# Graph attention on one NeuronCore: when the weighted sums and the expert network of a tile are issued

## The chip, the cores and the metric

The kernel runs on one core of a Trainium2 chip. Time is device microseconds (us) of one execution. Each of the core's engines works through its own queue in order: PE (matrix products; PEld is its weight load), DVE (vector operations), ACT (activation functions and copies), POOL (here it issues the indexed loads, "gathers") and SP (here it issues the plain transfers). Semaphores order one engine's work after another's. [...]

## The reference

A graph has 3125 nodes with 256 features and 50000 edges sorted by destination. Two blocks follow one another, each with a residual sum: a relational graph convolution with a mixture of 16 experts, and then the block that this change touches:

```python
x = x + _L1_gnn_ref(_layernorm(x), ...)          # two graph attention layers, 8 heads of 32
x = x + _L1_ffn_ref(_layernorm(x)[None], ...)[0] # shared MLP + 2 of 4 experts, chosen by a softmax gate
```

One attention layer takes h = x W; for each edge a score e = leaky_relu(a_s[src] + a_d[dst], 0.2), less the largest score of the edges with the same destination; z = exp of that; and for each destination the sum of z h[src] over its edges, divided by the sum of z, plus a bias. Between the two layers stands an ELU. The last network is a shared MLP (256-256-128-256), four experts (256-128-64-256, two chosen per node) and the gate.

## The kernel before

The last part of the kernel holds 25 tiles of 125 destination nodes. A tile's edges fill 17 columns of 128 edges (CT = 17), in three parts of 6, 6 and 5 columns (PARTS). `layer` runs the 25 tiles as steps s, and in a step it works on several tiles at once: `new` is tile s+1, `now` is tile s, `old` is tile s-1 and `older` is tile s-2. It is called twice, for layer one and layer two of the attention; both calls stand in `tc.manual_schedule()`, in which each engine takes the instructions in the order in which the code emits them. Instructions that stand outside such a block are placed by the scheduler where it finds room. So the table `sel`, whose `iota` for POOL (L2052) and whose first vector operation (L2054) come after the first layer in the code, are executed inside the first layer.

What a step does, with the names used below:

- `fetch(new)`: POOL issues 17 gathers of 128 rows of h (line L113, a helper) into tiles g0, g1, g2, three buffers each. `fetch_rows`: SP loads index rows and carries for a tile further on.
- `scans(now)`: ACT copies the gathered scores (L1821), DVE runs two scans for the largest score (L1824, L1825), PE turns the ends (L1828, L1829). `hot_rows(new)`: two long ACT operations (L1873, L1874).
- `one_hot(now)` (DVE, L1837) builds the 0/1 matrix of edge to destination; `destinations(now)` (DVE, L1833) sums the looked-up a_d; `carried(now)` (DVE, L1842 to L1848, then PE L1851) passes the largest scores across lanes; `lookup(new)` (PE, L1880); `scores(now)` (eight DVE operations L1856 to L1864, then ACT Exp L1866 and three copies L1868).
- `weighted(w, k)` multiplies part k of the gathered rows by z on DVE (L1886, in place); `summed(w, k)` adds the rows up by destination with PE (L1894). The matrix products are in float32, and the profile counts two for each.
- `means(old)` (DVE, L1900 to L1906) divides and adds the bias; then four tails. In layer one: `elu_parts` (ACT, L1991 to L1993), `elu_sum` (DVE L1996, then PE transposes L1967), `next_hidden` (ACT L2001, PE L1776) and `keep_next` (ACT L1782, the transfer L1783 that writes the row table which layer two gathers from, five small DVE operations L927 to L931). In layer two only the first does anything: `residual` (DVE L2066 to L2071, ACT L2073 and L2074).

Layer two also runs the last network on pairs of tiles, hooked into the steps by a lag: `run(s, (lag, stage))` runs the stage on pair (s-2-lag)/2 where that is a whole number. `first_layers` (two layers of the shared MLP and four experts, PE L2099, and the gate's product L2104, L2106; each layer is followed by an ACT relu L2085), `second_layers` (PE L2122, L2127), `spread` (PE L2178, L2183), `third_layers` (PE L2196), `finish` (DVE L2200, output transfer L2201), `gates`, `choice` and `shares` (some twenty small DVE operations with two ACT Exp between, L2110 to L2172), `shared_out` (DVE L2187) and `normalize` (DVE L2078, ACT Sqrt L2079, DVE L2080, ACT L2082).

Before the change, odd steps run `first_layers`, `gates`, `choice` and `shares`, and even steps run `second_layers`, `spread`, `third_layers`, `finish`, `shared_out` and `normalize`. What is left after the last step is in `last`. Where no tile is left, a stage is skipped; at s = 25 only `old` and `older` remain.

Of the kernel before, what the change touches and what calls it, by code (L numbers as in the profile page):

```python
# [45 lines left out]
def gnn_kernel(ctx: ExitStack, tc: tile.TileContext, a: dict, out: bass.AP):  # L46
# [834 lines left out]
    def by_tiles(ctx, start_i, hard):  # L881
# [880 lines left out]
        with ExitStack() as st:  # L1762
# [4 lines left out]
            fx = fixed.tile([128, 128 + D], F32, name="fx")  # L1767
            iota_ps, bias_ps = fx[:, :R], fx[:R, 128:]
            nc.vector.tensor_copy(iota_ps, iota_r[:, :R])
# [3 lines left out]
            def hidden(wx, xT):  # L1773
                p = ps.tile([R, D + 2 * H], F32, name="p_x")
# [78 lines left out]
            def scores(w):  # L1853

                es, bw, ep, ad_e = w.es, w.bw, w.pe[:, :2], w.pe[:, 2]
                nc.vector.tensor_tensor(ep, ends[:, w.t, :, None, :].to_broadcast([128, 2, H, CT]),  # L1856
                                        w.pc[:, :, :, None].to_broadcast([128, 2, H, CT]), OP.add)
                nc.vector.tensor_max(bw, bw, ep[:, 0])
                nc.vector.tensor_max(bw, bw, ep[:, 1])
                nc.vector.tensor_add(ep, es, ad_e[:, None].to_broadcast([128, 2, H, CT]))  # L1860
                nc.vector.tensor_scalar(es, ep, 0.2, None, op0=OP.mult)
                nc.vector.tensor_max(es[:, 0], es[:, 0], ep[:, 0])
                nc.vector.tensor_max(ep[:, 1], es[:, 1], ep[:, 1])
                nc.vector.tensor_sub(es[:, 0], es[:, 0], ep[:, 1])  # L1864
                w.z = ad_e.rearrange("q h i -> q (h i)").rearrange("q (i h) -> q i h", h=H)
                nc.scalar.activation(heads(w.z), es[:, 0], AF.Exp)  # L1866
                for g, (i0, i1) in zip(w.g, PARTS):
                    nc.scalar.copy(g[:, :, D:], w.z[:, i0:i1])  # L1868
# [19 lines left out]
            def summed(w, k):  # L1888

                if k == 0:  # L1890
                    w.p = ps.tile([R, DX], F32, name="p_sum")
                i0, i1 = PARTS[k]
                for i in range(i0, i1):
                    m = nc.tensor.matmul(w.p, w.oh[:, i, :], w.g[k][:, i - i0, :], start=(i == 0), stop=(i == CT - 1))  # L1894
                added[k].append(m.ins)
# [12 lines left out]
            def layer(h_tab, ad, bias, tail1, tail2, tail3, tail4, slot=None, mid=None, end=None, last=None):  # L1908
# [7 lines left out]
                for s in range(-1, T + 1):  # L1916
# [47 lines left out]
            def transposed(x):  # L1964
                p = ps.tile([128, 2, R], F32, name="p_x")
# [120 lines left out]

            def first_layers(u):
                n = u.n * R
                xT = pool.tile([128, 2, 2 * R], F32, name="xT2", bufs=2)
                for i in range(u.n):  # L2090
                    nc.scalar.copy(xT[:, :, i * R:(i + 1) * R], transposed(u.xc[:, i, :]))
                u.h1 = pool.tile([128, 2, 2 * R], F32, name="sh1")
                u.g1 = pool.tile([128, n_e, 2 * R], F32, name="eh1")
                for w, dst, bias in ([(s1[:, :, m * 128:(m + 1) * 128], u.h1[:, m, :n], b1[:, m:m + 1])
                                      for m in range(2)] +
                                     [(e1[:, e], u.g1[:, e, :n], eb1[:, e:e + 1]) for e in range(n_e)]):
                    p = ps.tile([128, 2 * R], F32, name="p_x")
                    for k in range(2):
                        nc.tensor.matmul(p[:, :n], w[:, k, :], xT[:, k, :n], start=(k == 0), stop=(k == 1))  # L2099
                    relu(dst, p[:, :n], bias)  # L2100
                u.pg = ps.tile([R, 2, n_e], F32, name="p_x")
# [14 lines left out]
            def second_layers(u):  # L2116
# [3 lines left out]
                p = ps.tile([128, 2 * R], F32, name="p_x")  # L2120
                for k in range(2):
                    nc.tensor.matmul(p[:, :n], s2[:, k, :], u.h1[:, k, :n], start=(k == 0), stop=(k == 1))  # L2122
                relu(u.h2[:, :n], p[:, :n], b2)
                for half in range(2):
                    p = ps.tile([128, 2 * R], F32, name="p_x")
                    for k in range(2):
                        nc.tensor.matmul(p[:, :n], e2[:, 2 * half + k, :], u.g1[:, 2 * half + k, :n],  # L2127
                                         start=(k == 0), stop=(k == 1))
                    relu(u.g2[:, half, :n], p[:, :n], eb2[:, half:half + 1])
# [44 lines left out]
            def spread(u):  # L2174
                n = u.n * R
                p = ps.tile([n_e + 1, 2 * R], F32, name="p_x")
# [4 lines left out]
                u.pw = ps.tile([128, 2, 2 * R], F32, name="p_x")  # L2181
# [7 lines left out]
            def third_layers(u):  # L2189
                u.po = ps.tile([R, 2, D], F32, name="p_x")  # L2190
# [25 lines left out]
            def mid(s):  # L2216
                run(s, (4, finish), (1, gates))

            def end(s):
                run(s, (2, shared_out), (0, normalize), (1, choice), (1, shares))  # L2220

            def last():

                u, v, w = pairs[-3:]
                for step, p in ((third_layers, u), (finish, u), (first_layers, v), (normalize, w), (gates, v),
                                (second_layers, v), (choice, v), (shares, v), (first_layers, w), (gates, w),
# [5 lines left out]
            with tc.manual_schedule():  # L2232
                layer(tabs[1], ads[1], biases[1], residual, *[lambda w: None] * 3, slot, mid, end, last)
# [43 lines left out]
```

## Time and profile before

| what | value |
|---|---|
| median of 12 runs | 2643.36 us (2635.28 to 2649.27) |
| the profiled execution | 2629.63 us, of which the span is 2628.0 |
| granted PE clock, mean over the span | 0.867 |
| busy in the span: PE, DVE, ACT, POOL | 74%, 52%, 30%, 53% |
| gathers of attention layer one on POOL | from 1433.25 us of the span to 1968.4 |
| first gather of layer two | 2010.94 us |
| last gather of layer two | 2544.03 us |
| scans of the last tile of layer two | 2557.03 us |
| last operation of DVE | 2621.33 us |

The profile is one execution. Its times count from the first instruction. A line of a timeline gives the start, the duration (of the whole row where xN says several), engine, line of the code, operation, output and input names and, in brackets, how long the engine was idle before and what ended the wait. "issue" means that nothing that the profile shows was waited for.

### The profile page before, as it was taken

The numbers are of one execution on the slowest core, as the hardware profiler recorded it, in microseconds if no ns is written. First come the engines' busy times: TensorE is split into PE (matmuls) and PEld (weight loads), VectorE is DVE, ScalarE is ACT, GpSimd is POOL, SyncE is SP. The second block draws the span as 40 slices with busy tenths as digits, with TensorE's granted clock in tenths as the row PEclk, the third lists the DMA queues.
The fourth block names the chain that finished last, engine by engine and source line by source line (L and its number), as shares of the span: only waits on it lengthen the run. The fifth ranks groups of instructions, "written<-read, shape, count | busy, mean of one in ns | idle before, by whom it ended". The sixth has DMA issues, their size and how long they took to land.

```text
span 2628.0 us, 26960 instructions
## 1 busy us (share of the span) xinstructions
PE 1954.8 (74%) x8604; PEld 1426.9 (54%) x8604; DVE 1370.0 (52%) x2950; ACT 799.3 (30%) x1699; POOL 1396.6 (53%) x1445
## 2 busy tenths in 40 slices
PE   6667879999564999997985266666653578888887
PEld 2234545555443878886863144444442366666665
DVE  4068863332451441132114377777763677878783
ACT  2221122222021242242223233333331354445542
POOL 1106555775677704120015777777772777777750
PEclk9788999999776999998995588888886788989999
DMA  6524434554336737674634555555551554545430
GB/s 216 206 97 140 138 117 166 199 193 168 107 105 196 233 123 247 197 211 131 200 110 105 158 139 141 140 146 143 139 147 46 134 133 131 148 127 152 134 103 16
DMA packets 192309, 386.35 MB, mean 147 GB/s; under 512 B 39900, under 2 KB 112588, under 8 KB 186659
## 3 DMA queue, kind: packets, MB, share of 16 engines
q0 software_dynamic: 76464, 189.38, 27.6%
q1 hardware_dynamic: 104543, 184.41, 20.7%
q10 hardware_dynamic: 11152, 10.75, 1.2%
q8 instruction: 71, 1.16, 0.2%
q14 instruction: 79, 0.65, 0.1%
HBM read 294.45 MB, written 89.87 MB: 146 GB/s over the span
## 4 chain that ended last, share of the span: by engine, by line
PE 47%; DVE 17%; DMA 11%; POOL 11%; issue 9%; ACT 5%; SPq 0%; ACTq 0%; POOLq 0%; DVEq 0%
POOL g L113 10%; PE ph L1574 10%; PE p_tr L1266 10%; PE p_sum L1894 6%; PE sum L985 6%; PE py L1584 5%; DMA table_t<-tr 4%; DMA g<-h_tab_t,src_t 3%; PE p_x L2099 3%; DVE oh L1837 2%; DVE g L1886 2%; PE p_x L1776 1%; DMA g<-table_t,rg_t 1%; DVE to_lane L1165 1%; DMA xc<-xs_t 1%
## 5 line engine op out<-in xcount | busy, mean ns | idle before, releaser
L113 POOL DMA_INDIRECT g<-h_tab_t,src_t x850 | 808.6, 951 | 321.8 <-issue 265.6
L113 POOL DMA_INDIRECT g<-table_t,rg_t x450 | 447.7, 995 | 335.5 <-issue 114.8
L1894 PE MATMUL p_sum<-g,oh 128*125 128x264 f32 x1700 | 462.9, 432 | 14.4 <-DVE g L1886 11.7
L1894 PEld LDWEIGHTS p_sum<-g,oh 128*125 128x125 f32 x1700 | 356.3, 214 | 95.6 <-DVE g L1886 13.1
L1266 PE MATMUL p_tr<-w_rel_t,xT_t 128*125 128x512 f32 x800 | 370.8, 619 | 43.6 <-ACT tr L1269 43.6
L1574 PE MATMUL ph<-xcT,w 128*128 128x256 f32 x1312 | 310.6, 385 | 0.7 <-ACT xcT L1566 0.7
L985 PE MATMUL sum<-g,oh 128*125 128x256 f32 x900 | 240.5, 420 | 62.9 <-DMA g<-table_t,rg_t 29.4
L1266 PEld LDWEIGHTS p_tr<-w_rel_t,xT_t 128*125 128x125 f32 x800 | 155.3, 197 | 232.2 <-issue 176.2
L1886 DVE TENSOR_TENSOR g<-g,p_e 128x1536 f32<-128x1536 f32 x150 | 244.9, 1661 | 46.4 <-ACT g L1868 24.4
L1574 PEld LDWEIGHTS ph<-xcT,w 128*128 128x128 f32 x1312 | 249.3, 193 | 34.1 <-ACT xcT L1566 1.1
L1578 DVE TENSOR_TENSOR hT<-silu,ph 128x256 f32<-128x256 f32 x164 | 68.8, 420 | 378.4 <-ACT silu L1577 378.3
L1269 ACT COPY tr<-p_tr 125x512 f32<-125x512 f32 x200 | 115.0, 586 | 485.6 <-PE p_tr L1266 396.1
L985 PEld LDWEIGHTS sum<-g,oh 128*125 128x125 f32 x900 | 182.6, 208 | 110.7 <-issue 56.5
L113 POOL DMA_INDIRECT y<-ys,pos_i x50 | 61.2, 1224 | 330.3 <-DMA ys<-yc 218.7
L1584 PE MATMUL py<-w,hT 128*128 128x256 f32 x656 | 156.8, 382 | 0.2 <-DVE hT L1578 0.2
L1000 DVE TENSOR_TENSOR xr<-xr,sum 125x256 f32<-125x256 f32 x75 | 31.4, 418 | 240.5 <-PE sum L985 198.8
L1577 ACT ACTIVATE silu<-ph 128x256 f32<-128x256 f32 x164 | 62.7, 383 | 237.7 <-PE ph L1574 237.7
L1584 PEld LDWEIGHTS py<-w,hT 128*128 128x128 f32 x656 | 124.3, 191 | 17.2 <-DVE hT L1578 0.6
L1967 PE MATMUL p_x<-ident,en 125*128 125x125 f32 x50 | 16.7, 436 | 142.8 <-DVE en L1996 142.8
L1837 DVE TENSOR_TENSOR oh<-lo_t,fx 128x2125 f32<-128x2125 f32 x50 | 117.1, 2343 | 0.0
L1866 ACT ACTIVATE p_e<-es 128x136 f32<-128x136 f32 x50 | 14.4, 287 | 326.9 <-DVE es L1864 326.9
L1873 ACT ACTIVATE rows<-rows,minus_p 125x2176 bf16<-125x2176 bf16 x50 | 105.2, 2105 | 26.1 <-DMA g<-h_tab_t,src_t 17.5
(341 smaller groups left out, 2476.2 us busy)
## 6 DMA issues: line engine op xcount, KB each, us to landing
w<-in_L_ffn_w SPq DMA_DIRECT2D x123, 512.0 KB
table_t<-tr SPq DMA_DIRECT2D x44, 1000.0 KB
rows<-lo_rows_t SPq DMA_DIRECT2D x50, 531.2 KB
g<-h_tab_t,src_t POOLq DMA_INDIRECT x850, 2.9
xc<-xs_t SPq DMA_DIRECT2D x41, 256.0 KB
ys<-yc ACTq DMA_DIRECT2D x41, 256.0 KB
xs_t<-zero SPq DMA_DIRECT2D x9, 1024.0 KB
g<-table_t,rg_t POOLq DMA_INDIRECT x450, 5.3
```

Source lines behind the costliest of these rows:

```text
L113: return nc.gpsimd.indirect_dma_start(out=dst, out_offset=None, in_=table, in_offset=bass.IndirectOffsetOnAxis(ap=idx, axis=0))
L985: m = nc.tensor.matmul(r.p[:R, :D], r.oh[k][:, i - i0, :], r.g[k][:, i - i0, :], start=(i == r.parts[0][0]), stop=(i == r.parts[1][1] - 1))
L1266: m = nc.tensor.matmul(p, xT[:, k, t * R:(t + 1) * R], w_rel[:, k, r0:r0 + 2, :].rearrange("p r o -> p (r o)"), start=(k == 0), stop=(k == 1))
L1269: nc.scalar.copy(tr[:, 2 * q * D:(2 * q + 2) * D], p)
L1574: nc.tensor.matmul(p[:, which, :], u.w12[:, which, k, m * 128:(m + 1) * 128], u.xcT[:, k, :], start=(k == 0), stop=(k == 1))
L1578: nc.vector.tensor_mul(u.hT[:, m, :], s, p[:, 1, :])
L1584: nc.tensor.matmul(u.py[:, j, :], u.hT[:, m, j * 128:(j + 1) * 128], u.w3[:, m, :], start=(m == 0), stop=(m == nh - 1))
L1837: nc.vector.tensor_tensor(w.oh, lo[:, w.t, :, None].to_broadcast([128, CT, R]), iota_ps[:, None, :].to_broadcast([128, CT, R]), OP.is_equal)
L1873: nc.scalar.activation(w.rows, w.rows, AF.Abs, bias=minus_p[:R, :])
L1886: nc.vector.tensor_mul(g, g, w.z[:, i0:i1, :, None].to_broadcast([128, i1 - i0, H, HD]))
L1894: m = nc.tensor.matmul(w.p, w.oh[:, i, :], w.g[k][:, i - i0, :], start=(i == 0), stop=(i == CT - 1))
L2099: nc.tensor.matmul(p[:, :n], w[:, k, :], xT[:, k, :n], start=(k == 0), stop=(k == 1))
```

## The change

Attention: `weighted` and `summed` of a tile, which stood in the tile's own step (the last product one step later), all move into the next step. Part 0 stands between `one_hot` and `carried` there, parts 1 and 2 between `carried` and `destinations`. z no longer overwrites a part of the tile p_e; it gets its own place in the PSUM tile fx, in which the lane numbers (now in bf16) and the bias already lie. p_sum has one buffer instead of two, p_x three instead of two. The wait of the gathers on earlier sums names the tile three before.

Tails: `tail3` moves a step later, to just after `hot_rows`; `tail4` to after `tail1`, and `tail2` behind `tail4`.

Network: the transposes of `first_layers` become a stage of their own, `turned`. Odd steps now run `turned` (early), `shared_out` and `finish` (fill) and `first_layers` (slot). Even steps run `gates`, `choice` and `shares` (fill), `second_layers`, `spread` and `third_layers` (slot) and `normalize` (end). The output of two layers goes into one PSUM tile, all products of the two first, then the two relus.

```diff
-            iota_ps, bias_ps = fx[:, :R], fx[:R, 128:]
+            iota_ps, bias_ps = fx[:, :64].bitcast(BF16)[:, :R], fx[:R, 64:64 + D]
+            z_ps = fx[:, 64 + D:].rearrange("q (i h) -> q i h", h=H)
...
-                    if len(added[k]) >= 3:
-                        after_all(rows[0], [added[k][-3]])
+                    if w.t >= 3:
+                        after_all(rows[0], [added[k][w.t - 3]])
...
-                w.z = ad_e.rearrange("q h i -> q (h i)").rearrange("q (i h) -> q i h", h=H)
+                w.z = z_ps
...
-                    w.p = ps.tile([R, DX], F32, name="p_sum")
+                    w.p = ps.tile([R, DX], F32, name="p_sum", bufs=1)
...
+                    if older:
+                        tail3(older)
+                    if early and now:
+                        early(s)
                     if now:
                         one_hot(now)
-                        destinations(now)
-                    if older and s < T:
-                        tail4(older)
+                    if old:
+                        weighted(old, 0)
+                        summed(old, 0)
                     if now:
                         carried(now)
                     if old:
-                        summed(old, 2)
+                        for k in (1, 2):
+                            weighted(old, k)
+                            summed(old, k)
+                    if now:
+                        destinations(now)
+                    if fill:
+                        fill(s)
                     if new:
                         lookup(new)
                     if now:
                         scores(now)
                     if slot and now:
                         slot(s)
-                    if now:
-                        weighted(now, 0)
                     if old:
                         means(old)
                         tail1(old)
+                    if older:
+                        tail4(older)
+                    if old:
                         tail2(old)
+                    if s == T:
                         tail3(old)
-                    if now:
-                        summed(now, 0)
-                        weighted(now, 1)
-                        summed(now, 1)
-                        weighted(now, 2)
-                    if s == T:
-                        tail4(older)
                         tail4(old)
-                    if mid and now:
-                        mid(s)
                     if end and now:
                         end(s)
...
+            def turned(u):
+                n = u.n * R
+                p = ps.tile([128, 2, 2 * R], F32, name="p_x", bufs=3)
+                for i in range(u.n):
+                    for k in range(2):
+                        nc.tensor.transpose(p[:, k, i * R:(i + 1) * R], u.xc[:, i, k * 128:(k + 1) * 128], ident[:R, :R])
+                u.xT = pool.tile([128, 2, 2 * R], F32, name="xT2", bufs=2)
+                nc.scalar.copy(u.xT[:, :, :n], p[:, :, :n])
...
+                for c in range(0, len(made), 2):
+                    p = ps.tile([128, 2, 2 * R], F32, name="p_x", bufs=3)
+                    for j, (w, _, _) in enumerate(made[c:c + 2]):
+                        for k in range(2):
+                            nc.tensor.matmul(p[:, j, :n], w[:, k, :], xT[:, k, :n], start=(k == 0), stop=(k == 1))
+                    for j, (_, dst, bias) in enumerate(made[c:c + 2]):
+                        relu(dst, p[:, j, :n], bias)
...
-            def mid(s):
-                run(s, (4, finish), (1, gates))
+            def early(s):
+                run(s, (1, turned))
+
+            def fill(s):
+                run(s, (2, gates), (2, choice), (2, shares), (3, shared_out), (5, finish))
 
             def end(s):
-                run(s, (2, shared_out), (0, normalize), (1, choice), (1, shares))
+                run(s, (0, normalize))
```

In `last`, `turned` stands ahead of each `first_layers`; the order is otherwise the same, but for `normalize` of the last pair, which now stands ahead of the first layers of the pair before it.

More of the change, by code (lines that the diff above doesn't have):

```diff
@@ L1773, in hidden @@
             def hidden(wx, xT):
-                p = ps.tile([R, D + 2 * H], F32, name="p_x")
+                p = ps.tile([R, D + 2 * H], F32, name="p_x", bufs=3)
                 for k in range(2):
@@ L1906, in means, with layer @@
                 nc.vector.tensor_add(w.v, w.v, bias_ps)
-            def layer(h_tab, ad, bias, tail1, tail2, tail3, tail4, slot=None, mid=None, end=None, last=None):
+            def layer(h_tab, ad, bias, tail1, tail2, tail3, tail4, early=None, fill=None, slot=None, end=None,
+                      last=None):
                 nc.vector.tensor_copy(bias_ps, bias)
@@ L1964, in transposed @@
             def transposed(x):
-                p = ps.tile([128, 2, R], F32, name="p_x")
+                p = ps.tile([128, 2, R], F32, name="p_x", bufs=3)
                 for k in range(2):
@@ L2175, in spread @@
                 n = u.n * R
-                p = ps.tile([n_e + 1, 2 * R], F32, name="p_x")
+                p = ps.tile([n_e + 1, 2 * R], F32, name="p_x", bufs=3)
                 for i in range(u.n):
@@ L2189, in third_layers @@
             def third_layers(u):
-                u.po = ps.tile([R, 2, D], F32, name="p_x")
+                u.po = ps.tile([R, 2, D], F32, name="p_x", bufs=3)
                 for i in range(u.n):
@@ L2214, in slot @@
                 run(s, (1, first_layers), (2, second_layers), (2, spread), (4, third_layers))
-            def mid(s):
-                run(s, (4, finish), (1, gates))
+            def early(s):
+                run(s, (1, turned))
+            def fill(s):
+                run(s, (2, gates), (2, choice), (2, shares), (3, shared_out), (5, finish))
             def end(s):
-                run(s, (2, shared_out), (0, normalize), (1, choice), (1, shares))
+                run(s, (0, normalize))
             def last():
                 u, v, w = pairs[-3:]
-                for step, p in ((third_layers, u), (finish, u), (first_layers, v), (normalize, w), (gates, v),
-                                (second_layers, v), (choice, v), (shares, v), (first_layers, w), (gates, w),
+                for step, p in ((third_layers, u), (finish, u), (turned, v), (normalize, w), (first_layers, v), (gates, v),
+                                (second_layers, v), (choice, v), (shares, v), (turned, w), (first_layers, w), (gates, w),
                                 (spread, v), (shared_out, v), (choice, w), (shares, w), (second_layers, w),
@@ L2232, in by_tiles @@
             with tc.manual_schedule():
-                layer(tabs[1], ads[1], biases[1], residual, *[lambda w: None] * 3, slot, mid, end, last)
+                layer(tabs[1], ads[1], biases[1], residual, *[lambda w: None] * 3, early, fill, slot, end,
+                      last)
     tiles = ctx.enter_context(tc.tile_pool(name="tiles", bufs=1))
```

32 lines of the change are left out of this document (14 added, 18 removed).

## The prediction

> **What bounds the kernel now.** I read first the groups of POOL over the stretch of layer two (its gathers, with mean and idle time), then the timeline.
>
> ```profile
> L113 POOL DMA_INDIRECT g<-h_tab_t,src_t x425 | 403.4, 949 | 173.1 <-issue 154.3 <-PE p_sum L1894 4.3 <-PE p_x L2099 1.9
> ```
>
> A gather takes 0.95 us, and 0.30 of "issue" stands before nearly each: 17 per step make 17 x 1.25 = 21.3 us. No change to the other engines alters that. The timeline shows the ends of the layer:
>
> ```profile
> 2010.94 0.94 POOL L113 DMA_INDIRECT g<-h_tab_t,src_t  x1 [42.52 <-issue]
> ...
> 2034.08 0.44 DVE L1824 TENSOR_TENSOR_SCAN fw<-cut_ft,es 128x136 f32<-128x136 bf16 x1 [25.89 <-ACT es L1821]
> ...
> 2544.03 0.95 POOL L113 DMA_INDIRECT g<-h_tab_t,src_t  x1 [0.30 <-issue]
> ...
> 2557.03 0.43 DVE L1824 TENSOR_TENSOR_SCAN fw<-cut_ft,es 128x136 f32<-128x136 bf16 x1
> ```
>
> POOL never stops from 2010.94 to 2544.98, 21.36 a step. DVE starts tile 0 at 2034.08; at POOL's pace tile 24 would start 24 x 21.36 later, at 2546.7. It starts at 2557.03. So layer two lags POOL by 10.3 us at its end, and that is all that a better order of the steps can win. From step 3 (2098.11) to step 24 lie 458.9 us, 43.7 for a pair of steps against 42.7 of POOL. Layer one has no lag left: its last tile waits for its gathers at 1971.27.
>
> The end of an even step in layer two, and the waits of DVE in layer two (2098 to 2557):
>
> ```profile
> 2266.42 0.15 DVE L2071 TENSOR_SCALAR ln_st<-ln_st 125x1 f32<-125x1 f32 x1
> 2266.61 0.51 ACT L2073 ACTIVATE ln_xc<-xr,ln_st 125x256 f32<-125x256 f32 x1 [0.28 <-DVE ln_st L2071]
> 2266.69 3.15 DVE L1886 TENSOR_TENSOR g<-g,p_e 128x1536 f32<-128x1536 f32 x2
> ...
> 2267.67 1.28 ACT L2079 ACT_TABLE_LOAD   x1
> ...
> 2273.27 0.21 ACT L2079 ACTIVATE ln_st<-ln_st 125x2 f32<-125x2 f32 x1 [4.31 <-DVE ln_st L2078]
> 2273.51 0.17 DVE L2080 RECIPROCAL ln_st<-ln_st 125x2 f32<-125x2 f32 x1 [0.27 <-ACT ln_st L2079]
> 2273.71 0.91 ACT L2082 ACTIVATE ln_xc<-ln_xc,ln_st 125x256 f32<-125x256 f32 x2 [0.23 <-DVE ln_st L2080]
> 2274.52 0.59 ACT L1821 COPY es<-g 128x48 f32<-128x48 f32 x3
> ```
>
> ```profile
> DVE fw L1824 <- ACT es L1821: 20.3, 11, 4.3
> DVE xr L2200 <- PE p_x L2196: 17.8, 9, 3.0
> DVE g L1886 <- ACT g L1868: 13.3, 17, 0.8
> ```
>
> ACT's residual work (1.05) and its table load (1.28) run beside the products L1886 and the additions, which the code puts behind the residual. The next scans wait for ACT's copies L1821, which stand behind all else of the step in ACT's queue.
>
> **The change part by part.** Step lengths are walked from rows of 2253 to 2298, each taken from the start of one operation to that of the next: scans 0.83, one_hot 2.26, product 0 1.67, carried 1.45, products 1 and 2 3.15, destinations 0.49, scores 3.04, means 1.35, residual 1.06, finish 0.61, shared_out 0.58, gates with choice and shares 4.55.
>
> Even step of layer two: DVE without finish and shared_out sums to 19.85. Then nothing is left for DVE but normalize, whose cover, the products, has gone to the next step. ACT works alone: start 0.05, L2073 and L2074 1.05, table load and its gap 1.29, Sqrt with handoff 0.27, reciprocal 0.20, L2082 to the copies 0.81, copies to the scans 0.63. Together 4.30: 24.15.
>
> Odd step: DVE sums to 16.5, so PE and ACT set it. Product 0 ends at 4.85. PE then does sum 0 (12 products of 0.234, by 5.61 for 24), the carry's transposes (0.35), sums 1 and 2 (22 more) and lookup (0.65), with 0.3 for the first handoffs, to 14.1. first_layers takes 5.35 (2241.91 to 2247.25), to 19.45; its last two relus 1.0; only then, in ACT's order, L2073 and L2074 (1.05) and the copies (0.63): 22.15. Two layers in a PSUM tile spare PE nothing here: its 24 products already ran at 0.22 each; and three p_x buffers are free in time.
>
> PE of the even step ends 1.2 us into the odd one (third_layers 4.2 behind ACT's copy L2180), where its next wait is at 4.85; nothing is lost. The pair is 46.3, over POOL's 42.7, so POOL will wait. Steps 3 to 23 are 11 odd and 10 even: 243.7 + 241.5 = 485.2, that is +26.3.
>
> Bounds: an odd step not under POOL's 21.36 and, with sums at layer one's rate (6.52 for 24), not over 24.4; an even one not under 21.36, if ACT's chain is covered after all, and not over 25.4, if a second table load (1.28) is exposed. I take the walks, all of whose terms are rows of this stage; half way to each end gives pairs of 44.5 to 48.1, -19 to +19 us over the 10.5 pairs.
>
> What the load costs shows at 2595.78: 1.28, and the Exp behind it starts at 2597.07, 0.01 later. So 1.29 stands in the sum. [...]
>
> z, bias and lanes in one bank: L927 waits for L1782, read against read of one p_x, so DVE and ACT are kept apart there. The bias addition comes 0.8 after the scores, z's copies end then: between nothing and 0.1 a step, under ACT's tail; I take nothing. bf16 lanes: the one-hot L975 reads such lanes from PSUM, 406 ns for 250 elements and 669 for 500; 2125 elements give 2.38 against 2.34, which is off the path; I take nothing.
>
> Layer one: DVE does 15.7 and waits 1.2 for elu_parts; PE's sums end at 13.4; so steps end near 17, under 21.3, and stay hidden by POOL. SP: the write of h (L1783) moves from 2 us to some 16 us into the step, and the index rows queue behind it. They are wanted a step later, over 20 us, and the slow load issued at 1932.27 landed after 8.7. Nothing. The output transfer leaves SP earlier in the pair. Nothing.
>
> POOL: a buffer's sum now comes a step later. With no lag part 0's sum ends 8 us into a step, and the gather that needs its buffer is due at 18.6 (21.3 less 2.7 for the landing): 10 us to spare. Not in step 1:
>
> ```profile
> 1480.05 0.44 DVE L1824 TENSOR_TENSOR_SCAN fw<-cut_ft,es 128x136 f32<-128x136 bf16 x1 [3.15 <-ACT es L1821]
> 1499.45 0.28 DVE L2054 TENSOR_SCALAR sel_lt<-sel 5x256 f32<-5x256 f32 x1 [18.96 <-POOL sel L2052]
> ```
>
> DVE waits 19 us there for POOL's iota, behind 51 gathers. Now tile 0's sum, needed by the gather of tile 3 (due 1499.6), is queued behind that wait: scan and one_hot to 1502.3, product to 1504.0, 12 matrix products at 0.325 (7.79 for 24 at 1473.89) to 1508.0, restart 1508.3: +8.7 for POOL and all that follows. If L2054 is placed elsewhere, 0. I take 8.7, the place of before.
>
> Between the layers: before, 39.7 us from 1971.27 to 2010.94. After, scans, one_hot, product and sum 0 of tile 23, transposes, sums 1 and 2 end at 14.5; means 16.0, elu_parts 17.2, the older tile's L1782 and its five operations 18.6, elu_sum 19.0, transposes and copy 20.0, hidden 22.2, tile 24's 34 products (8.6) 30.9, means 32.2, elu_parts 33.4, the five operations with their copy 34.85, elu_sum 35.3, transposes and copy 36.3, hidden 38.5, then 4.2 as now: 42.7. +3.0, between +1 and +5.
>
> End: before 71.0 from the last scans to the end. After: step 24 ends on DVE at 22.7 with the reciprocal; PE does third_layers to 25.4 and tile 24's sums to 33.5, third_layers to 37.6, transposes, first_layers from 39.05 (before 30.4) to 44.4. From there 34.3 to DVE's last addition before; two layers per tile and a third p_x buffer take off the waits on relus near 2588 and 2611, about 5.6, and the rest is as now: 74, +3; between -4 with all covers and +8 with no relus saved.
>
> Sum: 8.7 + 3.0 + 26.3 + 3 = +41.0. The profiled 2629.63 becomes 2670.6. It lies 13.7 under the median; on the median 2684.4.
>
> **Rivals.** (1) No wait at step 1: the scheduler puts L2054 behind tile 0's product. For it: the code only orders it after the iota. Against: the same POOL queue up to there. 2675.7.
> (2) Not slower: the order takes the exposed ACT tail off, both steps fit POOL's 42.7 and the 10.3 lag goes. For it: DVE's own work is 36.4 a pair. Against: ACT's copies L1821 are last in its queue, with 4.3 of chain ahead. Price -10.3, +3.0 between the layers, -4 at the end, none at step 1: 2632, faster. It decides at even steps under 21.4.
> (3) The pair stays at 43.7, with no wait at step 1 and the end as before: +3.0, 2646, the same.
> (4) PE is colder between its bursts and odd steps reach 24.4: 11 x 2.25 = 25 more, 2709.
>
> **How the numbers follow.** The walk as summed 0.50 (own range 2668 to 2700), rival 1 0.24, rival 2 0.08, rival 3 0.06, rival 4 0.06, pairs of 44 to 44.5, 2650 to 2656, 0.06. Range 2652 (pairs of 44.2, no wait at step 1: 26.3 - 10.5 x 2.1 = 4.3, 3.0 between, 1 at the end: +8.3) to 2704 (the walk with +8 at the end and odd steps 1.3 longer); some 0.15 lie below, 0.06 above. Under 0.2% (5.3 us, what a measurement tells from no change) counts as the same: faster 0.08, same 0.06, slower 0.86.
>
> **What would show it.** Right: in layer two POOL's gathers wait for p_sum; pairs near 46; behind the residual of even steps DVE idle some 4 us until L1821, with the table load in it; in odd steps idle 5 us; in layer one at 1499 a gather waiting 8 us. Wrong: POOL without waits and steps of 21.4, or L1821 done before the residual's ACT work.

## The result, and the profile after

The changed kernel takes 2680.51 us (median of 8 runs, 2671.33 to 2685.68), the kernel before 2642.55 in the same comparison: a ratio of 1.0138 with a 95% interval of 1.0121 to 1.0155. The predicted 2684 and its range hold. The profiled execution of after has a span of 2670.72 against 2627.96, which is 42.8 us more. The medians differ by 38.0 us; the other 4.8 are spread of single executions, as the profiled one of before lies 12.9 under its median and that of after 8.1.

Read first where POOL stands in layer two. The groups of POOL from 2020 to 2584 us of the changed kernel (busy time, mean ns, idle time before them) and the two ends of the layer in its timeline:

```profile
L113 POOL DMA_INDIRECT g<-h_tab_t,src_t x425 | 406.0, 955 | 202.6 <-issue 178.4 <-PE p_sum L1897 5.5 <-ACT ge L2131 4.7
```

```profile
2020.60 0.95 POOL L113 DMA_INDIRECT g<-h_tab_t,src_t  x1 [44.76 <-issue]
...
2043.80 0.44 DVE L1827 TENSOR_TENSOR_SCAN fw<-cut_ft,es 128x136 f32<-128x136 bf16 x1 [26.01 <-ACT es L1824]
...
2583.45 0.95 POOL L113 DMA_INDIRECT g<-h_tab_t,src_t  x1 [0.30 <-issue]
...
2597.15 0.44 DVE L1827 TENSOR_TENSOR_SCAN fw<-cut_ft,es 128x136 f32<-128x136 bf16 x1 [4.74 <-ACT es L1824]
```

Before, POOL's gathers of layer two took 533 us from the first to the last; now they take 563 (2020.60 to 2583.45). Added over the gathers, what they waited beyond the usual gap of 0.30 grew from 3.4 to 30.6 us: one wait of 1.8 to 3.0 us in 13 of the 24 steps, at a tile's first gather, where by the code it waits for the sum of the tile three before (the profile puts most of these waits down to "issue"). POOL no longer sets the pace, the steps do. Why they are long stands at the end of an even step, in the timeline of ACT and DVE:

```profile
2291.59 0.15 DVE L2078 TENSOR_SCALAR ln_st<-ln_st 125x1 f32<-125x1 f32 x1
...
2291.94 0.50 ACT L2080 ACTIVATE ln_xc<-xr,ln_st 125x256 f32<-125x256 f32 x1
...
2293.00 1.28 ACT L2086 ACT_TABLE_LOAD   x1
2293.01 0.17 DVE L2085 TENSOR_SCALAR ln_st<-ln_st 125x2 f32<-125x2 f32 x1 [1.26 <-ACT ln_sq L2081]
2294.29 0.21 ACT L2086 ACTIVATE ln_st<-ln_st 125x2 f32<-125x2 f32 x1
2294.53 0.17 DVE L2087 RECIPROCAL ln_st<-ln_st 125x2 f32<-125x2 f32 x1 [1.35 <-ACT ln_st L2086]
2294.73 0.91 ACT L2089 ACTIVATE ln_xc<-ln_xc,ln_st 125x256 f32<-125x256 f32 x2 [0.24 <-DVE ln_st L2087]
2295.55 0.60 ACT L1824 COPY es<-g 128x48 f32<-128x48 f32 x3
...
2296.18 0.44 DVE L1827 TENSOR_TENSOR_SCAN fw<-cut_ft,es 128x136 f32<-128x136 bf16 x1 [1.48 <-ACT es L1824]
```

DVE ends its residual at 2291.74 and starts the next scans at 2296.18. In the 4.44 us between, ACT works alone, but for two DVE operations of 0.17, through the residual, the table load, the square root and the scaling, and the copies L1824, for which the scans wait, come last. Before, the products lay beside the first half of that chain.

From step 3 to step 24 of layer two lie 488.9 us (458.9 before): even steps take 24.12 (before 21.70), odd ones 22.51 (before 22.00). The 42.8 us are: 3.5 by which layer one starts later, 6.2 from its first gather to layer two's (583.9 against 577.7), 0.5 up to step 3, 30.0 in the steps, 2.6 from step 24 to the end (73.6 against 70.9).

### The profile page after: what moved, and what is told of

Its sections match the earlier page's. It is cut to its first block, busy times and chain, and to the rows that moved or that the text cites. A ratio compares the mean times of both kernels' runs of the same rounds, so it can differ in the third digit from the quotient of the medians.

```text
span 2670.7 us, 27155 instructions
## 1 busy us (share of the span) xinstructions
PE 1991.8 (75%) x8604; PEld 1442.8 (54%) x8604; DVE 1363.5 (51%) x2951; ACT 788.1 (30%) x1687; POOL 1402.2 (53%) x1445
## 5 line engine op out<-in xcount | busy, mean ns | idle before, releaser
L1897 PE MATMUL p_sum<-g,oh 128*125 128x264 f32 x1700 | 487.6, 450 | 78.8 <-issue 45.0
L1897 PEld LDWEIGHTS p_sum<-g,oh 128*125 128x125 f32 x1700 | 371.8, 223 | 173.2 <-issue 55.1
L1266 PE MATMUL p_tr<-w_rel_t,xT_t 128*125 128x512 f32 x800 | 374.6, 623 | 42.3 <-ACT tr L1269 42.3
L1889 DVE TENSOR_TENSOR g<-g,fx 128x1536 f32<-128x1536 f32 x150 | 243.8, 1650 | 0.3
L1869 ACT ACTIVATE fx<-es 128x136 f32<-128x136 f32 x50 | 14.4, 287 | 396.6 <-DVE es L1867 392.6
L1831 PE MATMUL p_c<-ident,fw 128*8 128x128 f32 x100 | 26.6, 363 | 122.1 <-DVE fw L1827 122.1
```

The costliest lines, as they stand in the source:

```text
L1266: m = nc.tensor.matmul(p, xT[:, k, t * R:(t + 1) * R], w_rel[:, k, r0:r0 + 2, :].rearrange("p r o -> p (r o)"), start=(k == 0), stop=(k == 1))
L1889: nc.vector.tensor_mul(g, g, w.z[:, i0:i1, :, None].to_broadcast([128, i1 - i0, H, HD]))
```

## The experiments

They were run in four series, each with its own runs of the kernel before. In the second and fourth series that kernel took 3313.59 and 3298.51 us instead of 2640, on other chips; ratios of these series are not set against those of the others.

### One half of the change alone

`e1_attention_only`: the new order of the attention, with the network's stages where before has them.

```diff
-            def early(s):
-                run(s, (1, turned))
-            def fill(s):
-                run(s, (2, gates), (2, choice), (2, shares), (3, shared_out), (5, finish))
             def slot(s):
-                run(s, (1, first_layers), (2, second_layers), (2, spread), (4, third_layers))
+                run(s, (1, turned), (1, first_layers), (2, second_layers), (2, spread), (4, third_layers))
             def end(s):
-                run(s, (0, normalize))
+                run(s, (4, finish), (1, gates), (2, shared_out), (0, normalize), (1, choice), (1, shares))
```

> The new order of the attention alone: gates, choice, shares, finish and shared_out stand at the end of the steps again, as before the change; two layers per PSUM tile stay. Theory (in layer two the steps of the changed kernel are set by what stands uncovered behind the residual: ACT's chain in even steps, PE then ACT in odd ones): the gates then wait, uncovered, for the end of first_layers (some 23 us into the odd step) and take 4.6 more, and finish waits for third_layers in even steps, so odd steps of 27 us, even ones of 26, from step 3 to step 24 some 560 us against 489 in the changed kernel and 459 before: a time near 2750. Rival (the move of the network stages is what costs): 2640 to 2650.

`e2_network_only`: the attention of before (z, lanes and bias too stand where before has them), with the network's stages in their new places, two layers per PSUM tile (a tile in the memory that PE writes) and the changed numbers of p_sum and p_x buffers. The edit against before, in part:

```diff
                         hot_rows(new)
+                    if early and now:
+                        early(s)
...
                         summed(old, 2)
+                    if fill:
+                        fill(s)
...
-                    if mid and now:
-                        mid(s)
                     if end and now:
                         end(s)
```

> The new places of the network stages alone, in the old order of the attention (products in their own step, so that two thirds of them stand behind the residual and cover ACT's work). Theory: odd steps need 17.5 us of DVE, even ones 22.9, a pair under POOL's 42.7, so the lag of 10 us of the kernel before all but goes: some 9 us less than before, 2633. Rival (the network's move costs): 2660 or more. Rival (two layers per tile or the single p_sum buffer cost): also over 2650.

Measured: the attention alone 2767.37 (one run), 124 us slower than before in its series; the network alone 2638.90, ratio 0.9995 [0.9982, 1.0008], no change. The waits of DVE in layer two (2110 to 2560; us in total, times, longest), first of the attention alone, then of the network alone:

```profile
DVE xr L2218 <- PE p_x L2214: 49.2, 7, 7.0
DVE gm L2127 <- PE p_x L2123: 47.1, 8, 5.9
DVE rd L1903 <- PE p_sum L1897: 30.3, 16, 2.2
```

```profile
DVE run L1842 <- PE p_c L1829: 29.7, 8, 4.6
DVE fw L1824 <- ACT es L1821: 28.9, 15, 4.7
```

With the attention alone nothing of DVE is left to lie beside the network's products, so DVE waits for `finish`'s and `gates`' inputs (L2218, L2127): even steps 27.4, odd ones 28.1. The 9 us expected of the network alone did not come. The waits for the additions did go (17.8 before), but `third_layers` at the end of an even step now delays the tile's own sums behind it: in one such step 24 of their products run from 2322.04 to 2329.43, in the odd step that begins at 2321.72, PE turns the scans' ends only behind them (2329.35), and the carry's scan waits (p_c, 29.7 in eight odd steps). The pair is 44.1 against 43.7. So the slowdown belongs to the attention's half of the change; the network's new places take back 87 of its 124 us. That half is the new order together with the new places of z, lanes and bias, which e2 does not have; e3 below keeps those places and is within 0.2 per cent of before, so what costs is the order. Two layers per PSUM tile and the single p_sum buffer are in e2 and cost nothing in sum.

### What stands ahead of the copies in ACT's queue

`e3_normalize_later`: `normalize` is split; its variance and square root (`spreads`) follow the next step's scans, its reciprocal and scaling (`scaled`) follow `one_hot`.

```diff
+                    if begin and now:
+                        begin(s)
+                    if now:
+                        one_hot(now)
+                    if early and now:
+                        early(s)
                     if new:
                         hot_rows(new)
                     if older:
                         tail3(older)
-                    if early and now:
-                        early(s)
-                    if now:
-                        one_hot(now)
+                    if turn and now:
+                        turn(s)
...
-            def early(s):
-                run(s, (1, turned))
+            def begin(s):
+                run(s, (1, spreads))
+            def early(s):
+                run(s, (1, scaled))
+            def turn(s):
+                run(s, (1, turned))
...
-            def end(s):
-                run(s, (0, normalize))
```

> The changed kernel with normalize moved from the end of even steps behind the scans of the next step (Sqrt ahead of one_hot, scaling behind it, and the long ACT operations after that). Theory: ACT's copies for the scans no longer stand behind the table load and the scaling; even steps 21.6 instead of 24.1, odd ones 22.7 instead of 22.5; 466 us from step 3 to step 24 instead of 489, some 23 us less than the changed kernel: 2657. Rival (even steps are long for their DVE work and the waits between products): even steps stay at 24, 2680.

`e4_residual_first`: in odd steps `means` and the residual stand ahead of `first_layers`, so that ACT's residual does not follow six relus.

```diff
-                    if slot and now:
+                    if slot and now and s % 2 == 0:
                         slot(s)
                     if old:
                         means(old)
                         tail1(old)
+                    if slot and now and s % 2:
+                        slot(s)
```

> The changed kernel with means and residual ahead of first_layers in odd steps, so that ACT does the residual's two operations before the relus and not after. Theory: odd steps one us shorter (21.5 in the mean), even ones as they are: 11 us less than the changed kernel, 2669. Rival (odd steps are set by DVE or by POOL): 2680.

Measured: e3 2646.95, ratio 1.0018 [1.0000, 1.0036]; e4 2661.06, ratio 1.0075 [1.0056, 1.0095]. In e3 even steps fall to 21.39 and the stretch of layer two to 457.6; POOL's waits there fall to 3.9. At the end of an even step of e3, DVE's timeline is this:

```profile
2329.79 0.15 DVE L2080 TENSOR_SCALAR ln_st<-ln_st 125x1 f32<-125x1 f32 x1
2331.56 0.44 DVE L1827 TENSOR_TENSOR_SCAN fw<-cut_ft,es 128x136 f32<-128x136 bf16 x1 [1.62 <-ACT es L1824]
```

Between the residual and the next scans lie 1.62 us, ACT's residual work and the copies, instead of 4.44; that is 2.8 less, and the even steps are 2.7 shorter. Moving one stage of ACT's queue wins back 1.2 of the 1.38 per cent: the exposed chain is shown to be the cause. The 2657 expected was 10 us too slow, mostly because odd steps came out at 22.16 and not 22.7. e4 leaves even steps at 24.11, as it should, but odd ones fall to 20.93, by 1.6 where one us had been expected, and the time is 8 us under the 2669 expected. The odd steps of the changed kernel explain the rest. Windows of such steps (length; PE, PEld, DVE, ACT, POOL busy; PE clock; DMA share and GB/s), of the changed kernel and then of e4:

```profile
2204.10:2225.20 21.10, 17.69 (x103) 14.27 (x101) 15.73 (x29) 10.40 (x22) 16.06 (x17) 1.00 0.49 133
2249.10:2272.00 22.90, 19.11 (x102) 15.05 (x100) 15.91 (x29) 10.59 (x22) 15.89 (x18) 0.93 0.47 129
2296.20:2319.90 23.70, 20.29 (x102) 15.88 (x100) 15.80 (x28) 10.33 (x21) 15.97 (x17) 0.86 0.45 131
```

```profile
2249.70:2269.90 20.20, 17.66 (x103) 14.30 (x101) 15.76 (x29) 10.24 (x22) 15.32 (x17) 1.00 0.49 135
2294.10:2314.20 20.10, 17.46 (x102) 14.16 (x100) 15.73 (x28) 10.14 (x21) 15.22 (x17) 1.00 0.48 130
```

The same instructions take 21.1 at a granted clock of 1.00 and 23.7 at 0.86. Against a step at full clock e4 wins 1.0, as expected; the rest is that seven of its eleven odd steps run at full clock, where four of the changed kernel's do.

### Layer one

`e9_layer_one_ahead`: `layer` gets both orders and a flag; layer one runs in that of before, layer two as changed.

```diff
+                    if ahead:
...
+                    else:
...
-                layer(tabs[0], ads[0], biases[0], elu_parts, elu_sum, next_hidden, keep_next)
+                layer(tabs[0], ads[0], biases[0], elu_parts, elu_sum, next_hidden, keep_next, ahead=True)
```

> Layer one in the order of before, layer two as changed. This takes away the wait in step 1 and the longer drain between the layers together. By the prediction's two terms 8.7 + 3.0: 2680.5 - 11.7 = 2668.8. By the trace of the changed kernel, where the two waits of the gathers come to about 2.8 and the drain to 2.6 over that of before: 2675. Layer two's pair of steps stays at 46.6 in both; if it moves, the two layers are coupled in a way that neither saw.

`e5_sel_early`: the lines that make `sel` stand ahead of the first layer.

```diff
+            sel = pool.tile([5, 2, 128], F32, name="sel")
...
+            nc.vector.tensor_mul(sel, sel, sel_lt)
             with tc.manual_schedule():
                 layer(tabs[0], ads[0], biases[0], elu_parts, elu_sum, next_hidden, keep_next)
```

> The changed kernel with the selector's iota and the three VectorE operations behind it (sel, sel_lt) issued ahead of layer one, so that no VectorE operation stands behind GpSimd's queue of gathers in step 1. By the prediction's term the wait cost GpSimd 8.7 us: 2680.5 - 8.7 = 2671.8. By the trace of the changed kernel, where the operation came to stand behind tile 0's first product and the gathers waited 1.40 and 1.97 us at 1512 and 1528 (0.30 of each is the usual gap), it is about 2.8: 2677.7, and the stretch of layer one's gathers shortens by that.

e9 took 2673.63, but against the runs of before in its series the ratio is 1.0137 [1.0110, 1.0163], that of the changed kernel: the times cannot tell a gain of 5 us here. The trace can: from the first gather of layer one to that of layer two 576.7 us instead of 583.9, so the new order costs layer one and the drain behind it 7 us, not the 11.7 predicted. Layer two gave 3.0 of it back (491.9 from step 3 to 24): its even steps are unchanged at 24.16, its odd ones 22.76 with one more of the long kind.

Why the wait in step 1 was cheaper than predicted, in the timeline of the changed kernel:

```profile
1486.77 1.75 DVE L1889 TENSOR_TENSOR g<-g,fx 128x1536 f32<-128x1536 f32 x1
...
1503.30 0.28 DVE L2061 TENSOR_SCALAR sel_lt<-sel 5x256 f32<-5x256 f32 x1 [13.91 <-POOL sel L2059]
...
1512.09 0.95 POOL L113 DMA_INDIRECT g<-h_tab_t,src_t  x1 [1.40 <-ACT g L1871]
...
1527.52 0.95 POOL L113 DMA_INDIRECT g<-h_tab_t,src_t  x1 [1.97 <-issue]
```

The first product of tile 0 (1486.77) now stands ahead of the waiting operation; only parts 1 and 2 stand behind it, and their buffers are wanted later. e5 ran in the second series (3271.37, ratio 0.9888 [0.9864, 0.9913]); there the gathers of layer one waited 158 us in all for other reasons, and a term of 3 us cannot be read from it. It stays inconclusive.

### The table load, and two layers per PSUM tile

`e6_two_more_loads`: an additional square root and exponential of two columns ahead of the Sqrt. What they give is not used.

```diff
                 nc.vector.tensor_scalar(v, v, 1.0 / D, EPS, op0=OP.mult, op1=OP.add)
+                more = small("more")[:, :u.n, 0]
+                nc.scalar.activation(more, v, AF.Sqrt)
+                nc.scalar.activation(more, more, AF.Exp)
                 nc.scalar.activation(r, v, AF.Sqrt)
```

> The changed kernel with an additional square root and an additional exponential of two columns ahead of each Sqrt of the normalization, so that ScalarE loads two more function tables there. By the trace a load is 1.28 us with the next operation 0.01 behind it, and such a small operation 0.21 to 0.26: 2 x 1.28 + 2 x 0.25 = 3.1 more on ScalarE's chain at the end of each even step, 27.2 in place of 24.1; 11 such steps in layer two's stretch and one or two at the end: +34 to +40, about 2718. [...] Second rival: the loads are covered by other work: 2681.

It ran in the second series (one run, 3278.85), so its time says nothing beside the expectation, but ACT's timeline at the end of an even step does:

```profile
2530.64 1.28 ACT L2087 ACT_TABLE_LOAD   x1
2531.94 0.20 ACT L2087 ACTIVATE more<-ln_st 125x2 f32<-125x2 f32 x1
2532.16 1.28 ACT L2088 ACT_TABLE_LOAD   x1
2533.45 0.20 ACT L2088 ACTIVATE more<-more 125x2 f32<-125x2 f32 x1
2533.66 1.28 ACT L2089 ACT_TABLE_LOAD   x1
2534.96 0.21 ACT L2089 ACTIVATE ln_st<-ln_st 125x2 f32<-125x2 f32 x1
```

Two switches add 3.02 us (2531.94 to 2534.96), 1.51 each with their small operation, where 3.1 had been expected. Even steps are 43.1 against the 40.1 of e5 on the same chip, which is the same 3.0.

`e7_one_layer_per_tile`, run again as `e7b_one_layer_per_tile`: the first and second layers with a PSUM tile for each layer.

```diff
-                for c in range(0, len(made), 2):
-                    p = ps.tile([128, 2, 2 * R], F32, name="p_x", bufs=3)
+                for w, dst, bias in made:
+                    p = ps.tile([128, 2 * R], F32, name="p_x", bufs=3)
...
```

> The changed kernel with one layer per PSUM tile again in the first and second layers of the networks, all else as changed (three p_x buffers, the new places). The prediction took it that two layers in a tile spare TensorE nothing in a step: 2681 within 5. Rival: the pairing lets TensorE run ahead of the relus; odd steps, which first_layers ends, grow by one more wait on a relu of 0.6 to 1.0 each in two places: +11 x 1.5 = 16, 2697.

> The changed kernel with one layer per PSUM tile again, all else as changed, on a chip where the kernel before takes 2640 us. The prediction took it that two layers in a tile spare TensorE nothing in a step: 2681 within 5, odd steps within 0.5 of the 22.5 of the changed kernel. Rival: the pairing lets TensorE run ahead of the relus; odd steps grow by 1.5: 2697.

They ran in the second and the fourth series: 3283.78, ratio 0.9927 [0.9902, 0.9952], and 3224.63, ratio 0.9755 [0.9721, 0.9790]. One kernel with two ratios 1.7 per cent apart: by the time, these chips cannot decide a question of 16 us. The traces answer part of it. The 24 products of the two first layers take PE 5.35 us in the kernel before, with one layer per tile, and 5.32 to 5.33 in every odd step from step 3 on of the changed kernel; in e7 and e7b they take 5.32 in step 23 (from 3185.27 and from 3145.91), which lies behind POOL's last gather and so is all but free of the waits told of in the last section. PE idles in none of these, and step 23 as a whole takes 20.7 us in e7 and 21.1 in e5 on the same chip, at a clock of 0.98 in both. So where results come in time the pairing spares PE 0.03 us in `first_layers`; what it does to the whole time was not measured on a chip where before takes 2640.

### Towards a faster kernel

`e8_both_moves`, run again as `e8b_both_moves`: the edits of e3, e4 and e9 together.

> Layer one in the order of before; layer two in the changed order with both earlier edits: the normalization split and moved behind the next step's scans, and in odd steps the means and the residual ahead of the first layers. If what the change lost lies in ScalarE's queue ahead of the next scans (layer two), in the drain between the layers and at the end, then layer two follows GpSimd at 21.36 a step with no lag: from 2646.95 with the one edit, -4 between the layers, -4 at the end, up to -8 of lag: 2631 to 2637, faster than before (2642.5). Rival: TensorE or VectorE is the next bound in layer two, the pair stays at 43.5 and only the drain is won back: 2643, the same as before.

> Layer one in the order of before; layer two in the changed order with the normalization split and moved behind the next step's scans, and in odd steps the means and the residual ahead of the first layers; on a chip where the kernel before takes 2640 us and not 3313. There what the change lost lies in ScalarE's queue ahead of the next scans, in the drain between the layers and at the end: -4 between the layers and -4 at the end from the 2647 with the one edit, and up to -8 of lag behind GpSimd: 2631 to 2637, faster than before. Rival: TensorE is the next bound, the pair of steps stays at 43.5, only the drain is won: 2643, the same as before. On a chip where TensorE's results come late, as where the kernel before took 3313, it is expected at 1.006 of the kernel before once more.

In the second series it took 3331.07, ratio 1.0062 [1.0044, 1.0080]; in the third 2635.57 against 2640.31, ratio 0.9982 [0.9962, 1.0001]. So it is 4.7 us faster by the medians, but the interval just reaches no change: a gain is not shown. Layer two is down to 454.2 from step 3 to step 24. What is left shows in two odd steps and in the beginning of the longer one:

```profile
2370.70:2390.90 20.20, 19.93 (x110) 15.56 (x108) 15.82 (x31) 12.58 (x25) 15.32 (x17) 1.00 0.48 136
2412.60:2436.80 24.20, 24.20 (x110) 18.12 (x108) 16.00 (x30) 12.66 (x25) 18.33 (x20) 0.79 0.47 134
```

```profile
2412.56 0.44 DVE L1827 TENSOR_TENSOR_SCAN fw<-cut_ft,es 128x136 f32<-128x136 bf16 x1 [1.62 <-ACT es L1824]
...
2419.78 0.68 DVE L1845 TENSOR_TENSOR_SCAN run<-cm,p_c 8x256 f32<-8x256 bf16 x1 [2.25 <-PE p_c L1832]
```

PE is busy for all of the longer step, and begins it with 6.2 us of `third_layers` left over from the even one, in which it had idled 3.55. It is not the only cause of long odd steps: in the one from 2194.7 (24.3 us at a clock of 0.98) ACT's copies at the end wait 4.0 us for a gather. `e10_third_early` moves `third_layers`:

```diff
-                run(s, (1, first_layers), (2, second_layers), (2, spread), (4, third_layers))
+                run(s, (1, first_layers), (2, second_layers), (2, spread))
...
-                run(s, (1, turned))
+                run(s, (1, turned), (4, third_layers))
...
-                run(s, (2, gates), (2, choice), (2, shares), (3, shared_out), (5, finish))
+                run(s, (2, gates), (2, choice), (2, shares), (3, shared_out), (4, finish))
```

> The kernel with both moves (layer one as before), and in even steps third_layers moved from the end of the slot to behind the scans, where TensorE idled 3.55 us (2392.35 to 2395.90), with its addition, finish, in the same step. In the kernel with both moves TensorE carried 6.2 us of third_layers over into the odd step (2412.56 to 2418.72), and was busy for all 24.2 us of it at a granted clock of 0.79. The theory is that this spill is what still lets odd steps exceed GpSimd's 21.36: odd steps 20 to 21.5 at either clock, even ones up to 22, the lag of 6 us behind the gathers gone or down to 2: 2630 to 2632, 0.996 to 0.997 of the kernel before. Rival: the even step's sums and scores are delayed by as much (TensorE fills its gap but the sums start 3 later and the means wait), no gain: 2636.

It ran only in the fourth series: 3259.42, ratio 0.9870 [0.9842, 0.9898]. The mechanism is there, in the timelines of DVE and PE at the start of an odd step:

```profile
2790.35 0.44 DVE L1827 TENSOR_TENSOR_SCAN fw<-cut_ft,es 128x136 f32<-128x136 bf16 x1 [16.90 <-ACT es L1824]
...
2790.94 0.59 PE L1831 MATMUL p_c<-ident,fw 128*8 128x128 f32 x2
```

In all odd steps from step 3 on PE turns the scans' ends 0.59 us after the scans start, where the kernel with both moves needed 3.3 to 6.2 in nine of eleven (e8b), and 6.2 to 8.5 in the second series (e8). Whether that makes the kernel faster than both moves alone where before takes 2640 was not tried. Nor can the gain over before be put down to these moves: e7b, which has none of them, gains more on the same chip (0.9755).

## Why the prediction was right, step by step

- **Even steps** (24.15): 24.12 measured. The chain of 4.30 that ACT runs alone is 4.44 in the rows above, and e3 shows that it is the cause: with its part from the table load on moved, even steps are 21.39.
- **The table load** (1.29, nothing behind it): right. In the rows above the square root starts 0.01 us after the load of 1.28 has ended (2293.00, 2294.29), and in e6 the next operation starts 0.01 to 0.02 after each of the three loads of 1.28.
- **Odd steps** (22.15, by PE and then ACT): the mechanism is right, as e4 shows, the size 0.36 short. There is no one length but three, 21.1, 22.9 and 23.7, by the clock that PE is granted; the walk, put together from rows of several steps, lies between them. This is the 3.7 us by which the steps exceed the 26.3 predicted. Rival 4, a colder PE with odd steps of 24.4, came near in four steps of eleven (23.7 to 23.8); the mean clock from step 3 to step 24 fell from 0.92 to 0.86.
- **The wait at step 1** (8.7): the one term that failed. The step "if L2054 is placed elsewhere, 0. I take 8.7, the place of before" was the wrong choice of the two: the scheduler put the operation behind tile 0's first product, so rival 1's condition held. Of the signs named, the gather waiting 8 us at 1499 did not come (the longest wait is 1.97); the 4.4 us behind the residual and the idle time at the end of an odd step (4.74 at 2597.15) did. POOL's additional waits in all of layer one grew only from 2.4 to 4.7 us.
- **Between the layers** (42.7): 42.3, from ACT's copies of the last tile to layer two's first gather. **The end** (+3): +2.6.
- **What it did not have**: layer one's first gather came 3.5 later. In the six kernels of the first and third series, which have the changed kernel's stages up to there, that gather starts anywhere from 1431.5 to 1440.9, so this is no more than the spread of single executions. The predicted +41.0 and the +42.8 of the profiles are therefore closer than their terms, and that is luck: 5.5 too much for layer one and the drain (11.7 against 6.2) was made up by 3.7 in the steps and 3.5 of spread. By the medians the change costs 38.0, so that 2680.5 lies between the walk (2684.4) and rival 1 (2675.7).
- **Two layers per tile spare PE nothing**: right for `first_layers` (5.35 against 5.32); the effect on the whole time is not settled.
- **Rival 2** (not slower, decided at even steps under 21.4) fell with 24.12. Its condition is what e3 makes (21.39), and e3 lands at 1.0018, still not faster: the order also costs the drain between the layers (44.6 against 39.7) and the end (75.8 against 70.9).

## What to carry to other kernels

An operation that waits for an engine's small copies waits for all that the engine's queue holds ahead of them: here the next scans start 4.44 us after DVE's last operation, and 1.62 with one stage of ACT's queue moved (e3). When work is moved away from beside a chain of small operations on two engines, walk that chain alone and see what comes last in its queue; here one stage put behind the consumer won back 32 us. And judge the two halves of a reordering apart: here one half alone cost 124 us and the other nothing, together they cost 38, so the halves do not add up and the change alone shows neither.

## What the runs showed of the hardware that was not expected

**PE's clock beats with the steps.** In the changed kernel odd steps from the seventh on come in turn as 21.1, 22.8, 23.7, 21.3, 22.7, 21.1, 22.6, 23.8, 21.1, by whether and when the clock drops to 0.50 around the 2.5 to 2.8 us in which PE has nothing to do. It does not drop in the steps of some 21.1; in those of some 22.7 it drops 1.1 to 1.3 us behind that gap, for 3.4 us; in those of 23.7 it drops within it (the gap from 2298.5 to 2301.1 in the slowest one shown), for 6.8 us, until 2306.5. With a pair 1.6 us shorter (e4) seven of eleven odd steps see no drop. From step 3 to step 24 all changes of the clock lie on one grid of 3.41 us; each stretch at 0.50 lasts 3.41, 6.83, 10.24 or 13.65 us. In the slowest step shown the clock fell some 1.2 us into the gap of 2.5 (the window from 2298 to 2300 has a mean of 0.92, so 0.3 us of it at half), and PE had been busy for two thirds of the 3.41 us before. What sets the moment of the fall these rows do not show.

**The end varies too.** From step 24 to the end e8b took 82.2 us in its profiled execution, the slowest of its twelve, against 72 to 74 in e4, e9 and the changed kernel: tile 24's 34 products took 10.2 us at a clock of 0.77, where they took 7.8 at 1.00 in e4. That is 2.4 us of the 8 to 10; the rest was not traced to a cause, but it is not the code alone, as the same kernel took 73.8 in e8, on another chip.

**Some chips are another machine for this kernel.** In the second and fourth series, with the same code, ACT stands still ahead of operations whose inputs PE's rows show as long done. In e5 the timeline of PE has the products of the shared MLP in `second_layers`, and that of ACT the relu behind them ("remote": what ended the wait is no instruction of the profile):

```profile
2513.77 1.09 PE L2139 MATMUL p_x<-sh,s 128*128 128x250 f32 x4
...
2528.89 0.47 ACT L2092 ACTIVATE sh<-p_x,b 128x250 f32<-128x250 f32 x1 [12.59 <-remote]
```

There are 18 such waits on that operation alone (252 us), mean steps of 37 (odd) and 40 (even), and the order of the kernels turns: e5, e7 and e10 beat before by 0.7 to 2.5 per cent, and e8 loses 0.6. These waits all but end with the gathers: in e5 the waits on "remote" come to 936 us, of which one of 3.1 lies behind POOL's last gather, and step 23, which starts behind it, takes 21.1 us as on the other chips; the traces of before, of the changed kernel and of e8b, on other chips, have none. Whether the gathers cause them was not tried. What holds the results, or the waiting engine, the rows do not show; it stays open.
